# A four-layer kernel on one core: six blocks of attention's result are turned by VectorE and a scratch array in DRAM instead of TensorE, and the last seven-product group gets a third PSUM tile and a last product in column halves

## The chip, the cores and the metric

The kernel runs on one core of one Trainium2 chip. The metric is the device time of one execution in microseconds (us). The kernel before takes 1473.97 us, the median of three runs (1473.82 to 1475.48).

## What is computed

Activations of 8 batches of 128 tokens, width 512, all in f32, pass four layers. Each layer adds `ffn(cond(x))` to `x`:

```
x = x + L0_ffn(L0_cond(x))     # gated FFN with LoRA; expert LoRA with a router
x = x + L1_ffn(L1_cond(x))     # two low-rank layers
x = x + L2_ffn(L2_cond(x))     # attention over a paged cache; linear + routed low-rank
x = x + L3_ffn(L3_cond(x))     # two more routed low-rank layers
```

The change lies where the third layer's attention ends, and at the very end. Attention (32 query heads, 8 key heads, head width 128, up to 512 cached keys and 128 new ones) gives `y2`, 1024 tokens x 512. What follows needs `y2` turned, with features on the partitions:

```
H = y2 @ W.T + b;  z = y2 @ A
logits, weights = from every second token's H[:, 0:8] and z @ LiMEs.T   # softmax, top 2
y3 = H + ((z * (weights @ LiMEs)) @ Bmat) * scaling
```

The last layer ends with a product of 1024 tokens x 512 by a 512 x 512 matrix, added to `x` and written out.

## The kernel before, in words

**Layout.** `x` stays in SBUF, features on partitions, [128, 4, 1024]. `y2` is the other way round: [128 tokens, 8 batches, 512].

**Attention** (`run`, L1364 on) goes in 32 steps, `n`: 8 groups of heads (`qd`), and in each four pairs of batches (`p`). Step `n` weighs its pair (`weigh`: scores `st`, exponentials `pT` on ScalarE), projects the pair of step n+1 (`project`), and puts the result of step n-1 through the output weights (`leave`: products `wo`, added to `y2` by VectorE and GpSimd). Matrix products are done by the seven-product scheme (seven block products in place of eight, the sums of blocks by VectorE). The sums of a step's exponentials are inverted and spread over the partitions through DRAM (`inverted`: SyncE's two DMAs `sums` and `R`), and `divided` (`oT`) uses them a step later. Keys and queries are turned by VectorE's 32x32 transposes, a DMA to DRAM (`written`, L1167, four DMAs each) and a DMA back (`kT`, L1165; `qT` and `kTn`, L1202 and L1204).

**The ending.** In the last group of heads (steps 28 to 31) the blocks of `y2` that are complete are turned. At the end of steps 29, 30 and 31, L1462 calls `end.turn` for the two batches of the pair before. `turn` (L1843) makes four TensorE transposes (L1849) into one PSUM tile `y2T` and one copy to SBUF (L1850: ScalarE for an odd batch, VectorE for an even one). The last two batches are turned in `layer2`, at its start.

`Y2T` feeds four things. `product` (the tiles `h`: four quarters of the tokens, q = 0 to 3; one product is 32 matmul records), `anchors` (`hdT`, then `hd`, every second token of all quarters), `low` (`z`), and through `anchors` the `routing`: a row of small VectorE, ScalarE and GpSimd operations (L1874 to L1944) that ends in `p`, which TensorE transposes in `gains` (`pT`, L1952). `product(0)` is called in `run` before the last `leave`; `layer2` calls anchors, product(1), routing, product(2), gains, and so on in that order.

**What sets the order.** Inside attention most instructions are held in the order in which they are written (`kept`, `tc.keep_in_program_order`). `turn` and `layer2` are not: there a scheduler at build time moves instructions on each engine by its own costs, and the order so found is fixed in the program. Each engine, SyncE's DMA queue too, runs its instructions in that order. Loads of the last two layers' weights (`open3`: `Bm`, `W`, `Wq`, `keys`, `wB3T`, `wmr`, `BwT`) are queued on SyncE behind step 31's DMAs.

**The end of the program** (`layer3`, `last`, class `Seven`). Four groups of seven products, 256 columns each; a group has two PSUM tiles (banks), `even` and `odd`, with two results in each. `last` adds the four results to `x` on VectorE (L2223) and sends each out by a DMA of SyncE (L2224). Then every engine reads a flag (`redo_i`, L814), branches over a part that is not run here (L815), and waits for the outstanding DMAs.

Of the kernel before, what the change touches and what calls it, by code (L numbers as in the profile page):

```python
# [10 lines left out]
F32 = mybir.dt.float32  # L11
I32 = mybir.dt.int32
AF = mybir.ActivationFunctionType
ALU = mybir.AluOpType
# [3 lines left out]
P = 128  # L18
NB = 8
NT = NB * P  # L20
D = 512
DC = D // P
# [25 lines left out]
def forward(ctx: ExitStack, tc: tile.TileContext, a: dict, out: bass.AP):  # L48
    nc = tc.nc
    pe, act, dve, pool, sp = nc.tensor, nc.scalar, nc.vector, nc.gpsimd, nc.sync  # L50

    def mm(o, lhsT, rhs, start, stop):
# [14 lines left out]
    x = xpool.tile([P, DC, NT], F32, tag="x", name="x")  # L67

    w3T, wB3T, A2T = (
        nc.dram_tensor(n, shape, F32, kind="Internal").ap()  # L70
        for n, shape in (("w3_turned", (D, D)), ("wB3_turned", (D, P)), ("A2_turned", (32, D)))
    )
# [5 lines left out]
    late_weights.append((  # L78
        a["A2"].rearrange("(c p) r -> p c r", p=P), A2T.rearrange("i (c q j) -> q i c j", q=4, j=32)
    ))  # L80
    late_turned = w3T, wB3T, A2T

    c0 = ExitStack()
    w0 = c0.enter_context(tc.tile_pool(name="w0", bufs=1))
# [36 lines left out]
    for k in range(7):  # L121
        n = 1 << k
# [214 lines left out]
    with c0:  # L337
# [73 lines left out]
        h = w0.tile([P, NF, NT], F32, tag="h", name="h")  # L411
# [157 lines left out]
        kept = tc.keep_in_program_order  # L569
        with tc.issue_after(rows_known.ins):  # L570
            for g in range(TG):
                token_sums(g)
            A = weight_sums(1, second, dve)
# [4 lines left out]
        for f in range(1, NF):  # L578
            after = f + 1 < NF and weight_sums(f + 1, gate_weights(f + 1))
            gates_by_seven(f, A, itertools.islice(tabled, 15) if f < 3 else itertools.islice(angles, 3))  # L580
            A = after
# [134 lines left out]
    with psa:  # L716
# [49 lines left out]
        kept = nc.dram_tensor("kept_x", (P, DC, NT), F32, kind="Internal").ap()  # L766
# [18 lines left out]
        y2, end = att.run(late, end_of, bank, lambda: sp.dma_start(kept, x))  # L785
# [29 lines left out]
    with tc.If(redo > 0):  # L815
        sp.dma_start(x, kept)
        y2 = attention_any(tc, a, x, ident, lens, kvrow, part, ww, wop, ypool, eps, rows, chunks, mm)
# [24 lines left out]
def attention(tc, a, x, ident, lens, kvrow, part, ww, wop, ypool, sums, rot, eps, psa, c2, chunks, mm):  # L842
# [6 lines left out]
    nc = tc.nc  # L849
# [517 lines left out]
    def run(pool_, end_of, bank, keep):  # L1367
        late.append(pool_)
        y2 = Y[0]
        squares(1, "q", 0, range(REP))  # L1370
        keys_terms = rotate(1)
        squared(1)
        keys_terms()
        roots(1)
        gather(2, "k")
        rotated(1)
        normed(1)
        end, prepared = None, iter(())
        w_ops, wo_ops = iter(()), WO[0].factors()

        def some(ops, k=1):
            return lambda: [next(ops, None) for _ in range(k)]

        for n, (qd, p) in enumerate(steps):

            after = n + 1 if 0 < n < len(steps) - 1 else None
            weigh(n, 0)
            sums_of, outs = added(n, 0), iter(())
            if n == 1:
                some(wo_ops, 2)()  # L1390
            next(sums_of)
            (some(wo_ops) if n == 1 else some(w_ops))()
            every(sums_of)
            every(w_ops)
            if n:
                divided(n - 1)
                outs = outputs(n - 1)
                if not after:
                    every(outs)
            if after:  # L1400
                project(after, {
                    "u2": lambda: every(outs),
                    "c22": lambda: (turn_cached(2)() if n == 1 else None, some(wo_ops, 3)()),
                    "c11": lambda: (squares(after, "k", 0, (0,)), squares(after, "q", 0, (0, 1))),
                    "c12": lambda: squares(after, "q", 0, (2, 3)),
                })
                keys_terms = rotate(after)
                if n + 2 < len(steps):
                    if steps[n + 2][1] == 0:
                        weights(steps[n + 2][0])  # L1410
                    gather(n + 2, "k")
                leave(n - 1, {
                    "one": lambda: (
                        squares(after, "q", 1, range(REP)), squares(after, "k", 1, (0,)), roots(after),
                    ),
                    "c22": lambda: (every(wo_ops), keys_terms(), rotated(after), normed(after), turn(after)),
                })
                fetch(after)
                gather(after, "v")
            mixed = mix(n, 0)  # L1420
            left = (lambda: leave(n - 1),) if n and not after else ()
            weigh(n, 1, {2: (some(mixed), *left), 3: (some(mixed),), 4: (some(mixed, NC),)})
            sums_of = added(n, 1)
            next(sums_of)
            summed(n, 0)
            if n == 0:
                next(sums_of)
                gather(1, "v")
            every(sums_of)
            if n == 0:  # L1430
                turn_at_once(1)
            summed(n, 1)
            if 0 < n < len(steps) - 2 and steps[n + 2][1] == 0:
                w_ops = W[steps[n + 2][0]].factors()
            inverted(n, some(w_ops))
            if n + 2 == len(steps):
                end.load_w2()
                end.load_aw()
            if left:
                end.shifted()  # L1440
            if n == 0:
                every(tokens(2))
            if n == 5:
                prepared = end.prepare(bank, lambda shape, name: wk.tile(shape, F32, tag="xs", name=name, bufs=1))
            next(prepared, None)
            every(mix(n, 1))
            next(prepared, None)
            if n and p == 0:
                out_weights(qd)
                wo_ops = WO[qd].factors()  # L1450
            if 0 < n < len(steps) - 2:
                turn_cached(n + 2)()
                some(w_ops)()
                every(tokens(n + 2))
            if n == 3:
                kept(keep())
            if n == 4:
                end = end_of(kept)

            if qd == NQ - 1 and p:  # L1460
                for j in range(2):
                    end.turn(y2, 2 * (p - 1) + j, bank)  # L1462
        divided(n)
        every(outputs(n))
        end.product(0, ("st", "st"), bank)
        leave(n)
        return y2, end
# [311 lines left out]
def ending(  # L1779
# [15 lines left out]
    def slot(j):  # L1795
        return slice(j * 32, (j + 1) * 32)
# [47 lines left out]
    def turn(y2, b, bank):  # L1844
# [4 lines left out]
            pe.transpose(ps[:, c, :], y2[:, b, c * P : (c + 1) * P], ident)  # L1849
        (act.copy if b % 2 else dve.tensor_copy)(Y2T[0][:, :, b * P : (b + 1) * P], ps)  # L1850

    def quarter(q):
        return slice(q * NT // 4, (q + 1) * NT // 4)

# [205 lines left out]
    class Seven:  # L2060


        def __init__(self, name, bank, A, B):
            self.A, self.B = A, B
            self.even, self.odd = (bank("mm", [P, 2, 256], f"{name}_{i}") for i in range(2))
            self.p1, self.u = (
                L3.w3.tile([P, 256], F32, tag=f"seven_{n}", name=f"{n}_{name}", bufs=2) for n in ("p", "u")
            )
            self.c = {(0, 0): (self.even[:, 0], None), (0, 1): (self.odd[:, 1], self.u),
                      (1, 0): (self.even[:, 1], self.u), (1, 1): (self.odd[:, 0], self.p1)}  # L2070

        def into(self, o, l, r, start=False):
            for c in range(2):
                mmq(o, l[:, c, :], r[:, c, :], start and c == 0, False)

        def begin(self):
            self.into(self.even[:, 0], self.A[0], self.B[0], True)
            act.copy(self.p1, self.even[:, 0])

        def go_on(self):  # L2080
            a11, a12, a22, s1, s2, s3, s4 = self.A
            b11, b21, b22, t1, t2, t3, t4 = self.B
            u, p1, even, odd = self.u, self.p1, self.even, self.odd
            self.into(odd[:, 1], s1, t1, True)
            self.into(odd[:, 0], s2, t2)
            dve.tensor_tensor(u, odd[:, 0], p1, ALU.add)
            dve.tensor_tensor(p1, odd[:, 1], p1, ALU.add)
            self.into(even[:, 1], s3, t3)
            dve.tensor_tensor(p1, even[:, 1], p1, ALU.add)
            self.into(odd[:, 1], s4, b22)  # L2090
            self.into(even[:, 0], a12, b21)
            self.into(even[:, 1], a22, t4)

    S = {}

# [107 lines left out]

    def last_begun(g, k, bank):

        f = S["o", g, k] = Seven(f"o3_{g}_{k}", bank, S["b"][k], S["z", g])
        f.begin()

    def last(g, k):
        f = S["o", g, k]  # L2210
        f.go_on()
        for (i, j), (ps, more) in reversed(f.c.items()):
            o = 2 * k + i
            tok = slice(g * 512 + j * 256, g * 512 + (j + 1) * 256)
            t = x[:, o, tok]
            if more is not None:
                dve.tensor_tensor(t, t, more, ALU.add)
        for ij in ((1, 1), (0, 1), (0, 0), (1, 0)):
            ps = f.c[ij][0]
            o = 2 * k + ij[0]  # L2220
            tok = slice(g * 512 + ij[1] * 256, g * 512 + (ij[1] + 1) * 256)
            t = x[:, o, tok]
            dve.tensor_tensor(t, ps, t, ALU.add)  # L2223
            sp.dma_start(out[o * P : (o + 1) * P, tok], t)  # L2224

    def layer2(y2, bank, do=range(NB)):

# [24 lines left out]
    def layer3(bank, between=lambda behind: None):  # L2252
# [35 lines left out]

    return SimpleNamespace(
        prepare=prepare, load_w2=load_w2, load_aw=load_aw, turn=turn,  # L2290
        product=product, shifted=shifted, open3=open3, layer2=layer2, layer3=layer3,
    )


# [63 lines left out]
```

## Time and profile before

One execution was profiled. It took 1478.06 us, 4.09 us (0.28%) above the median of the runs; the span that its trace covers, from the first instruction to the last, is 1476.2 us.

| what | value |
|---|---|
| median of the runs / profiled execution / its span | 1473.97 / 1478.06 / 1476.2 us |
| granted TensorE clock, mean | 0.998 |
| busy: TensorE, VectorE, GpSimd, ScalarE | 99%, 72%, 58%, 38% |
| DMA, mean over the span | 119 GB/s |
| end of attention's step 31 and ending up to `pT` | 1324.86 to 1360.38 us |
| last matmul ends / last VectorE addition ends / last instruction ends | 1469.17 / 1469.96 / 1476.2 us |

In the lines of the trace, `PE` is TensorE (`PEld` its loading of weights), `DVE` VectorE, `ACT` ScalarE, `POOL` GpSimd, `SP` SyncE; a `q` behind the name means the engine's queue, where its DMA issues, waits and branches lie. `L1849` is a line of the kernel. `out<-in` names tiles, with numbers left out. A row of the timeline has a start, a duration, engine, line, operation, tiles, shape and count; square brackets hold the idle time ahead of it and who ended it. A row of a group has the count, then the shortest, median and longest duration in ns, then the first and last start. Matmuls overlap, so a row's duration may be longer than the distance to the next one. The product of two 128-row blocks with 256 columns stands as two records, a transpose as one.

### The profile page before, as it was taken

How to read it: one execution, taken by the hardware profiler on the slowest of the kernel's cores; microseconds unless marked ns; L12 is line 12 of the kernel's file. 1: busy time of each engine (PE TensorE's matmuls, PEld its weight loads, DVE VectorE, ACT ScalarE, POOL GpSimd, SP SyncE). 2: the span in 40 equal slices, each digit the busy share in tenths (PEclk: the TensorE clock that was granted, in tenths of full speed). 3: DMA queues.
4: the chain of work that ended last, by engine and by line, in shares of the span. 5: the costliest groups of instructions: out<-in, count | busy, mean ns of one | idle time of the engine just before them, and what ended most of it. 6: DMA issues, size and time to landing. Idle time of an engine off the chain costs nothing.

```text
span 1476.2 us, 17664 instructions
## 1 busy us (share of the span) xinstructions
PE 1462.2 (99%) x5348; PEld 922.4 (62%) x5348; DVE 1063.5 (72%) x2125; ACT 561.2 (38%) x1421; POOL 851.1 (58%) x877
## 2 busy tenths in 40 slices
PE   9999999999999999999999999999999999999998
PEld 7888787455555555555565555555555555657886
DVE  4565534488888887777778777777878888875575
ACT  1111201044545544454554445445544444532110
POOL 2232104477767777777677777767777776731310
PEclk9999999999999999999999999999999999999999
DMA  7411222214645544564454455444445544343001
GB/s 244 121 44 33 47 42 68 91 38 118 183 152 170 155 118 125 156 182 127 138 151 119 125 155 180 133 138 147 116 131 154 170 143 135 113 121 99 1 16 45
DMA packets 168808, 175.09 MB, mean 119 GB/s; under 512 B 64544, under 2 KB 138528, under 8 KB 168576
## 3 DMA queue, kind: packets, MB, share of 16 engines
q1 hardware_dynamic: 150528, 136.86, 32.0%
q0 software_dynamic: 17056, 36.49, 7.9%
q8 instruction: 45, 0.74, 0.2%
q10 hardware_dynamic: 1120, 0.52, 0.1%
q14 instruction: 59, 0.48, 0.1%
HBM read 131.40 MB, written 42.14 MB: 118 GB/s over the span
## 4 chain that ended last, share of the span: by engine, by line
PE 95%; DVE 2%; DMA 1%; issue 1%; ACT 0%; SPq 0%; POOL 0%; DVEq 0%
PE st L1214 18%; PE av L1266 18%; PE g L381 9%; PE q_six L1020 8%; PE q_one L1020 6%; PE q_five L1020 6%; PE wo_two L1020 6%; PE dn L381 5%; PE wo_one L1020 4%; PE wo_six L1020 4%; PE eo_l L53 3%; PE h L1799 2%; PE z L1799 2%; PE midp_l L53 1%; PE o L1799 1%
## 5 line engine op out<-in xcount | busy, mean ns | idle before, releaser
L963 POOL DMA_INDIRECT kn<-in_k_cache,kvrow_k x256 | 272.0, 1062 | 77.3 <-issue 70.5
L963 POOL DMA_INDIRECT vals<-in_v_cache,kvrow_v x256 | 267.9, 1046 | 73.6 <-issue 60.5
L1266 PE MATMUL av<-pT,vals 128*128 128x512 f32 x640 | 290.6, 592 | 0.2 <-DVE oT L1276 0.2
L1218 ACT ACTIVATE pT<-st,hide 128x512 f32<-128x512 f32 x256 | 176.0, 688 | 186.9 <-PE st L1214 160.1
L1214 PE MATMUL st<-qT,kT 128*128 128x512 f32 x512 | 236.1, 594 | 1.3 <-issue 0.9
L1266 PEld LDWEIGHTS av<-pT,vals 128*128 128x128 f32 x640 | 121.4, 190 | 153.1 <-issue 148.0
L1119 POOL TENSOR_TENSOR vq<-q,txq 128x256 f32<-128x256 f32 x128 | 121.2, 978 | 137.6 <-ACT sqq L1093 97.9
L1214 PEld LDWEIGHTS st<-qT,kT 128*128 128x128 f32 x512 | 96.3, 190 | 111.6 <-issue 103.3
L1234 DVE TENSOR_TENSOR part<-pT 128x512 f32<-128x512 f32 x128 | 88.3, 691 | 77.1 <-ACT pT L1218 64.9
L1020 PE MATMUL q_one<-q,x 128*128 128x384 f32 x256 | 93.0, 486 | 0.0
L1093 ACT ACTIVATE sqq<-q 128x128 f32<-128x128 f32 x252 | 78.2, 310 | 10.4 <-DVE q L1069 3.7
L1020 PEld LDWEIGHTS q_one<-q,x 128*128 128x128 f32 x256 | 48.5, 190 | 39.8 <-issue 14.3
L1020 PE MATMUL q_six<-q_s,xs_all 128*128 128x384 f32 x192 | 69.8, 486 | 0.0
L1074 ACT COPY q<-q_one 128x256 f32<-128x256 f32 x32 | 11.9, 372 | 151.7 <-PE q_one L1020 133.4
L1020 PE MATMUL wo_one<-o,oT 128*128 128x256 f32 x256 | 65.8, 379 | 1.0 <-ACT k L1074 1.0
L1214 PE MATMUL st<-qT,kTn 128*128 128x512 f32 x128 | 65.4, 592 | 0.0
L1020 PE MATMUL wo_two<-o_s,os 128*128 128x256 f32 x256 | 60.5, 379 | 0.0
L1218 ACT ACTIVATE pT<-st,rs 128x512 f32<-128x512 f32 x64 | 44.0, 687 | 38.5 <-PE av L1266 22.6
L1020 PEld LDWEIGHTS wo_one<-o,oT 128*128 128x128 f32 x256 | 48.6, 190 | 14.7 <-issue 2.0
L450 POOL TENSOR_TENSOR ws<-wu 128x256 f32<-128x256 f32 (+1 forms) x9 | 6.4, 714 | 87.8 <-DMA wu<-in_WuT 80.1
L1250 ACT COPY rows<-rows 32x32 f32<-32x32 f32 x96 | 20.7, 216 | 92.8 <-DVE rows L1245 79.1
L381 PE MATMUL g<-xs,ws 128*128 128x256 f32 (+1 forms) x240 | 55.1, 379 | 0.0
(462 smaller groups left out, 2804.9 us busy)
## 6 DMA issues: line engine op xcount, KB each, us to landing
turned_new<-qkt SPq DMA_DIRECT2D x120, 160.0 KB
turned_cached<-kt SPq DMA_DIRECT2D x128, 128.0 KB
kT<-turned_cached SPq DMA_DIRECT2D x32, 512.0 KB
R<-sums SPq DMA_DIRECT2D x32, 512.0 KB
qT<-turned_new SPq DMA_DIRECT2D x30, 512.0 KB
q<-in_WqT SPq DMA_DIRECT2D x8, 1024.0 KB
o<-in_WoT SPq DMA_DIRECT2D x8, 1024.0 KB
kn<-in_k_cache,kvrow_k POOLq DMA_INDIRECT x256
```

What stands on the lines that cost most here:

```text
L53: pe.matmul(o, lhsT, rhs, start=start, stop=stop)
L381: pe.matmul(o, lhsT, rhs, start=start, stop=stop, skip_group_check=True)
L963: kept(pool.indirect_dma_start(out=d[:, c, :], out_offset=None, in_=kc if what == "k" else vc, in_offset=bass.IndirectOffsetOnAxis(ap=kvro ...
L1020: kept(pe.matmul(o, l[:, c, :], r[:, c, :], start=start and c == 0, stop=c == 1, skip_group_check=True))
L1093: kept(act.activation(sq, S[n][m][:, j, i, :], AF.Square, accum_out=S[n]["ssq"][:, j, col : col + 1]))
L1119: kept(pool.tensor_tensor(to, t[:, b, :, hi : hi + 64], wx[:, b, lo : lo + 64].unsqueeze(2).to_broadcast(list(to.shape)), ALU.mult,))
L1214: kept(pe.matmul(ps, s["kT"][:, c, 4 * j : 4 * j + 4, :] if c < 4 else s["kn"][:, j], s["qT"][:, :, REP * j : REP * (j + 1), :].rearrange( ...
L1218: kept(act.activation(pT[:, c, :, :].rearrange("p i t -> p (i t)"), ps, AF.Exp, **(dict(bias=hide[:, b, c : c + 1]) if c < 4 else dict(bia ...
L1234: kept(dve.tensor_tensor(o, l, r, ALU.add))
L1250: kept(act.copy(rows[0:32, g, :], rows[32 * g : 32 * g + 32, 0, :]))
L1266: kept(pe.matmul(ps, v[:, c, :], pT[:, c, :, :].rearrange("p i t -> p (i t)"), start=c == 0, stop=c == NC - 1, skip_group_check=True,))
L1799: return pe.matmul(o, lhsT, rhs, start=start, stop=stop, skip_group_check=True)
```

## The change

First part, the turning. For the pairs of steps 29, 30 and 31 the change calls a new `turned_in` in place of `turn`. For each of the two batches VectorE transposes a [128, 512] block in 32x32 squares to a tile in the buffers of the cached keys (`kn`), and SyncE writes it with four DMAs to an internal DRAM array; then four DMAs for each batch read it back into `Y2T`. All of it is held in its written order. The last two batches are turned as before.

```diff
+        def y2_turned(p):
+            bs = (2 * p, 2 * p + 1)
+            end.turned_in(y2, bs, lambda name: kvp.tile([P, 4, DC, 32], F32, tag="kn", name=name))
...
             if qd == NQ - 1 and p:
-                for j in range(2):
-                    end.turn(y2, 2 * (p - 1) + j, bank)
+                y2_turned(p - 1)
...
+    def turned_in(y2, bs, tile_of_turned):
+        if not Y2T:
+            Y2T.append(early.tile([P, DC, NT], F32, tag="yT", name="y2T"))
+        for b in bs:
+            t = tile_of_turned(f"y2t_{b}")
+            kept(dve.transpose(t, y2[:, b, :].rearrange("p (c k i) -> p k c i", k=4, i=32)))
+            for q in range(4):
+                kept(sp.dma_start(
+                    late_turned[3][b, :, :, q], t[32 * q : 32 * q + 32].rearrange("i k c j -> i (k c) j")
+                ))
+        for b in bs:
+            for k in range(4):
+                kept(sp.dma_start(
+                    Y2T[0][slot(k), :, b * P : (b + 1) * P],
+                    late_turned[3][b, :, DC * k : DC * (k + 1)].rearrange("i c a j -> i c (a j)"),
+                ))
```

Second part, the end. The group with `g + k == 2`, the last one, is built `apart`: its sixth product has a PSUM tile of its own, its last product is made in two halves of 128 columns, and the result of that product is added and sent out in two halves, one by SyncE, one by ScalarE. In every group `odd` is now allotted ahead of `even`.

```diff
+            self.odd = bank("mm", [P, 2, 256], f"{name}_1")
+            self.even = bank("mm", [P, 2, 256], f"{name}_0")
+            self.one, self.six = self.even[:, 0], (
+                bank("mm", [P, 2, 256], f"{name}_2")[:, 0] if apart else self.even[:, 1]
+            )
...
-            self.into(even[:, 0], a12, b21)
-            self.into(even[:, 1], a22, t4)
+            self.into(one, a12, b21)
+            for h in (slice(0, P), slice(P, 2 * P)) if self.apart else (slice(0, 2 * P),):
+                self.into(six[:, h], a22, t4[:, :, h])
...
-            dve.tensor_tensor(t, ps, t, ALU.add)
-            sp.dma_start(out[o * P : (o + 1) * P, tok], t)
+            n = P if f.apart and ij == (1, 0) else 2 * P
+            for h, by in zip(range(0, 2 * P, n), (sp, act)):
+                ps = f.c[ij][0][:, h : h + n]
...
+                dve.tensor_tensor(t, ps, t, ALU.add)
+                by.dma_start(out[o * P : (o + 1) * P, tok], t)
```

## The prediction

> **What bounds the kernel now.** I read the page first, its shares and its chain. The first line here is the page's busy time by engine, the second the chain of work that ended last.
>
> ```profile
> PE 1462.2 (99%) x5348; PEld 922.4 (62%) x5348; DVE 1063.5 (72%) x2125; ACT 561.2 (38%) x1421; POOL 851.1 (58%) x877
> ...
> PE 95%; DVE 2%; DMA 1%; issue 1%; ACT 0%; SPq 0%; POOL 0%; DVEq 0%
> ```
>
> TensorE has no gaps to fill. Work taken from it shortens the kernel, as long as no wait opens behind it. So: what do the turned blocks cost TensorE? From the groups by tile, then from the chain in order of time:
>
> ```profile
> L1849 PE MATMUL y2T<-ident,y x32: 272/273/273, 1273.9 to 1347.5; 128*128 128x128 f32 x32
> ```
> ```profile
> 1274.07 0.87 PE y2T L1849 x8
> ...
> 1307.19 0.87 PE y2T L1849 x8
> ...
> 1331.73 0.87 PE y2T L1849 x8
> ```
>
> A transpose lasts 273 ns, but eight stand on the chain with 0.87 us, 109 ns each. Third, TensorE's timeline where the ending begins, and of the same stretch the VectorE rows at the two ends of the routing:
>
> ```profile
> 1351.41 0.33 PE L1873 MATMUL hd<-ident,hdTs 128*128 128x128 f32 x1
> 1351.58 8.80 PE L1799 MATMUL h<-y2T,WT 128*128 128x256 f32 x40
> 1360.21 0.60 PE L1952 MATMUL pT<-ident,p 128*8 128x128 f32 x4
> ```
> ```profile
> 1351.78 0.22 DVE L1874 TENSOR_TENSOR hd<-hd,b 128x64 f32<-128x64 f32 x1 [1.10 <-PE hd L1873]
> ...
> 1357.56 0.19 DVE L1944 TENSOR_TENSOR p<-p,s 128x32 f32<-128x32 f32 x1
> ```
>
> The routing runs from 1351.74 (hd's end) to 1357.75, 6.0 us of small operations, and TensorE does not notice: 40 records of `h` (8.64 us on the chain) lie between `hd` and `pT`. This cover is what the change touches. Fourth, SyncE's rows of a write and its read back in step 29, and the end:
>
> ```profile
> 1275.35 1.91 SPq L1169 DMA_DIRECT2D turned_cached<-kt  x4
> 1281.11 0.34 SPq L1165 DMA_DIRECT2D kT<-turned_cached  x1
> ```
> ```profile
> 1469.20 0.76 DVE L2223 TENSOR_TENSOR x<-o,x 128x256 f32<-128x256 f32 x2 [0.76 <-PE o L1799]
> ```
> ```profile
> L815 SPq EVENT_SEMAPHORE  x8: 17/17/17, 1472.7 to 1474.5; - x8
> ...
> L815 ACTq EVENT_SEMAPHORE  x1: 17/17/17, 1461.1 to 1461.1; - x1
> ...
> L815 DVEq EVENT_SEMAPHORE  x1: 21/21/21, 1473.0 to 1473.0; - x1
> ```
>
> After 1470 only output DMAs and the closing of the program remain; SyncE's last DMA wait ends at 1474.5, and 1.7 us later all is over.
>
> **Turning: what is removed.** 24 transposes, 3 x 0.87 = 2.61 us of TensorE, all on the chain; three copies of 0.69 us on VectorE and three of 0.59 us on ScalarE, beside it. A rule speaks here: the Trainium skill (TensorE: Matmul & The Clock Gate, Part 4: PE-mode transpose) gives some 275 ns to a transpose within a kernel. The trace's duration agrees, 273 ns, but its spacing is 109 ns: by the rule 24 would be worth 6.6 us, by the row 2.61. I take the row, since only the spacing is TensorE's time here.
>
> **What is added.** Six VectorE transposes of 128x512, priced by `kt<-kn` (same shape and strides) at 0.71 us, two a step. In step 29 they come behind the `xs` sums that end at 1277.0 and hold up step 30's first addition of `part`: it was at 1277.42, may now start at 1276.6 and will at about 1278.2. VectorE had 1.32 us idle at 1287.02 for a product of TensorE, so this is made up before anyone needs it: nothing. In step 30 they run at 1304.7 to 1306.1, where VectorE sat idle until 1307.66: nothing. In step 31 VectorE waits 3.00 us for `R` anyway: nothing. Without that slack each pair would cost 1.4 us.
>
> 48 DMAs on SyncE, 16 a step, 64 KB each. Row for the trip: `turned_cached`, first write issued 1275.35, last issued by 1277.26, landed by 1281.11, so 3.9 us from last issue to landing. I take 0.44 us per issue (median of L1169), as much for a read (0.34 to 0.63, rows `R` and `kTn`), and 4.0 us to land (`R` of step 31: issued 1331.89, used 1335.90). A trip then is 3.5 + 3.9 + 3.5 + 4.0 = 15 us. Who is queued behind it on SyncE? Step 29: begins 1281.5, last read issued by 1292.4; next is `turned_new` at 1296.1. Step 30: behind `WT` and `AwT` (2 MB), reads done by about 1325; next is `sums` at 1328.8. Step 31: behind `R`, begins 1330.5, lands at 1345.4 (1347 with 0.63 a read); behind it the last layers' weights move from 1332.3 to about 1341, some 9 us later, `W` landing near 1348 where `qwp` wants it at 1360, `Bm` wanted at 1366, `wmr` at 1376: nothing. GpSimd's queue is not passed.
>
> **What is moved.** The built program of the changed kernel has another order on TensorE: product(1), which stood half before and half after `hd`, now lies wholly before it (it fills where the scheduler expects the late block), and between `hd` and `pT` there is only
>
> ```
> h_0 (product 2, first half) x8     in place of     h_0 x4, h_1 x8, h_0 x8
> ```
>
> that is 16 records in place of 40: 16 x 0.216 = 3.46 us in place of 8.64. In time: product(0) starts at 1332.61 - 2.61 = 1330.0. To `hd` TensorE has all it had, plus 24 records of `h` (5.18 us), less the short waits for copies of `y2T` it had there (0.2): `hd` ends at 1351.74 - 2.61 + 5.18 - 0.2 = 1354.1. Routing takes 6.0 again, with 0.1 to wake TensorE: `pT` starts at 1360.2. In the kernel before it starts at 1360.38 on the chain. Of 2.8 us gained some 2.65 become a wait at `pT`; **the turning brings 0.2 us**. From there the order is as before. First matmul that needs step 31's block: `hdT` at about 1350.9, more than 3.9 us after the late landing. If the cover were there, the gain would be the whole 2.8.
>
> **The end.** TensorE waited 0.18 us for VectorE's `p_o` at 1466.30; a product moved ahead of it (it no longer shares a bank) fills this: -0.18. The halves cost TensorE nothing: 8 records at 109 ns (the transposes' spacing, same columns) for 4 at 216. In the built program both halves' additions wait for the last matmul of both, so they do not overlap with it; but the addition of (0,0), which waited with (1,0) before, is now done earlier. After the last matmul there remain two additions of 128x128 (row `vals`, 0.28 us, 0.2 to 0.34 apart), about 0.5 in place of 0.76: together VectorE ends 0.45 earlier, near 1469.5. SyncE's last four issues ran from 1468.14 to 1471.78, with one of 1.58 and one of 0.81 us; the last was ready at 1469.96 and issued from 1470.97. Now SyncE has the same four, the last ready sooner, and ScalarE, idle, issues the other half at once. The Trainium skill (DMA: Bandwidth & Descriptors, Issuing engines are not separate DMA queues) says a second issuer saves only issue time; that is all I count. If SyncE's slow issue stays, its last ends at about 1471.2 (gain 0.6), else at 1469.8 (gain 2.0). ScalarE becomes a new candidate: after its DMA it reads the flag (0.47) and branches; its branch took from 1458.6 to 1461.1, so it is through at 1473.0, not 1461.1, against SyncE's 1474.5 before: no more than 1.5 to gain. I take **1.1 us**, bounds 0 and 2.0; the ends differ by SyncE's slow issue, which no row explains.
>
> **The sum.** 0.2 + 1.1 = 1.3 us. Against the profiled execution: 1478.06 - 1.3 = 1476.8, span 1474.9. Its 4.1 us over the median are outside the sum; from the median, 1473.97 - 1.3 = 1472.7.
>
> **Rivals.** *The cover holds.* Routing ends earlier than I think, or TensorE finds the missing 2.6 us. For: VectorE and ScalarE are almost idle there. Against: the row of operations is serial, and the order is fixed. Then 2.8 + 1.1: 1470.1. *Slower: the turned block is late.* Step 31's trip lands late at `hdT`, and everything behind, routing and `pT` too, moves with it, us for us. For: the 512 KB `R`, 128-byte squares and 8 reads queue on one issuer behind a receipt. Against: 4 to 5 us of slack. It decides above 1352.2, where the 1.3 us are eaten; at 1355, 4.1 us after 1350.9, the time is 1476.8 to 1477.5. *The end gives nothing:* the slow issue falls on the last DMA, or ScalarE's branch comes last: 1473.8. *The change does not do what it says* is excluded for the transposes (gone from the built order), and holds for the halves' overlap, as said.
>
> **How the numbers follow.** Likeliest, 0.65: 1472.7. Cover holds 0.15, late block 0.10, dead end 0.10. Range 1470.2 to 1475.6: at its low end the cover with little of the end, at its high end a late block of 3 us. Faster or slower by over 0.2% (2.9 us, about what a measurement of this kernel can tell from no change): faster 0.15 (the cover), slower 0.10 (late block), within 0.75.
>
> **What would show it.** Profile after: no `y2T` on TensorE before 1340; product(0) at about 1330.0; `hd` near 1354; before `pT` an idle of 2.6 us put down to VectorE's `p`; `pT` near 1360. If idle lies before `hdT` and names a DMA, the late block is right; if `pT` starts near 1357.6, the cover held. SyncE: `turned_new` not later than before. End: ScalarE's row after the branch near 1473, last addition near 1469.3. I am wrong if a wait appears in steps 29 to 31, above all for `qT` or `R`, which I priced at nothing.

## The result and the profile after

The changed kernel takes 1477.24 us, the median of 22 runs (1472.62 to 1480.26), beside 1474.59 us for the kernel before on the same chip (22 runs). The ratio is 1.0015, with a 95% interval of 1.0009 to 1.0021: it is slower by about 2.2 us (the medians differ by 2.65), and the forecast was 1472.7 us. The profiled execution took 1479.46 us with a span of 1477.7 us.

The two executions drift against each other: ahead of anything that the change touches, the one after already runs 1.1 us earlier (the first scores with new keys of step 29, `st<-qT,kTn`, stand at 1266.18 before and at 1265.08 after). So I measure from that row, called K below, and not from the start of the span. `1360.19` after is K + 95.11; `1360.21` before is K + 94.03.

TensorE's work fell, as meant. The first fence is the page's busy time, the second the groups of tile `y2T`: eight transposes are left of 32, and 24 reads of the scratch array are new.

```profile
PE 1460.3 (99%) x5328; PEld 919.6 (62%) x5328; DVE 1066.9 (72%) x2129; ACT 559.5 (38%) x1418; POOL 853.3 (58%) x877
```
```profile
L1869 SPq DMA_DIRECT2D y2T<-y_turned x24: 309/432/501, 1286.1 to 1338.6; - x24
L1853 PE MATMUL y2T<-ident,y x8: 272/272/273, 1344.4 to 1346.4; 128*128 128x128 f32 x8
```

SyncE's rows of step 31 show the trip through DRAM: writes from 1329.51, reads until 1339.02, and the median read lands 2.1 us after its issue, so the block is there at about 1341.1, over 5 us ahead of `hdT` at 1346.62.

```profile
1329.08 0.34 SPq L1260 DMA_DIRECT2D R<-sums  x1
1329.51 5.35 SPq L1864 DMA_DIRECT2D y_turned<-y2t  x8
1335.37 3.65 SPq L1869 DMA_DIRECT2D y2T<-y_turned  x8
```

TensorE's timeline of the ending; below it, VectorE's first and last row of the routing.

```profile
1344.36 0.38 PE L1853 MATMUL y2T<-ident,y 128*128 128x128 f32 x2
...
1346.62 0.42 PE L1803 MATMUL hdT<-y2T,WH 128*32 128x128 f32 x4
1346.97 0.70 PE L1803 MATMUL h<-y2T,WT 128*128 128x256 f32 x2
1347.60 0.63 PE L1803 MATMUL z<-y2T,A 128*32 128x256 f32 x4
1348.16 2.86 PE L1803 MATMUL h<-y2T,WT 128*128 128x256 f32 x12
1350.94 0.99 PE L1803 MATMUL hdT<-y2T,WH 128*32 128x128 f32 x26
...
1353.71 0.33 PE L1895 MATMUL hd<-ident,hdTs 128*128 128x128 f32 x1
1353.88 3.62 PE L1803 MATMUL h<-y2T,WT 128*128 128x256 f32 x16
1360.19 1.01 PE L1974 MATMUL pT<-ident,p 128*8 128x128 f32 x4 [2.69 <-DVE p L1966]
1361.13 1.94 PE L1803 MATMUL qwp<-W,Wq 128*32 128x512 f32 x8
```
```profile
1354.08 0.23 DVE L1896 TENSOR_TENSOR hd<-hd,b 128x64 f32<-128x64 f32 x1 [1.68 <-PE hd L1895]
...
1359.85 0.19 DVE L1966 TENSOR_TENSOR p<-p,s 128x32 f32<-128x32 f32 x1
```

Three things are to be seen. Product(1) lies ahead of `hd`, mixed with `hdT` and `z`, and only 16 records lie behind it. TensorE then waits 2.69 us for VectorE's `p`. And after the wait the same instructions take nearly twice their time: `pT` 1.01 us in place of 0.60, `qwp` 1.94 (before: 1.07). The stretches of 1 us say why. Behind the length of a stretch stand the busy times of TensorE, its weight loads, VectorE, ScalarE and GpSimd; the third number from the right is the granted clock of TensorE.

```profile
1359.00:1360.00 1.00, 0.00 (x0) 0.00 (x0) 0.86 (x5) 0.00 (x0) 0.00 (x0) 1.00 0.00 0
1360.00:1361.00 1.00, 0.81 (x4) 0.37 (x4) 0.04 (x1) 0.00 (x0) 0.00 (x0) 0.57 0.00 0
1361.00:1362.00 1.00, 1.00 (x8) 0.22 (x11) 0.00 (x0) 0.57 (x1) 0.00 (x0) 0.50 0.00 0
1362.00:1363.00 1.00, 1.00 (x12) 0.34 (x8) 0.00 (x0) 0.00 (x0) 0.74 (x2) 0.50 0.06 16
1363.00:1364.00 1.00, 1.00 (x21) 0.41 (x14) 0.04 (x1) 0.75 (x2) 1.00 (x2) 0.72 0.00 0
```

A mean of 0.57 means half the clock for 0.86 us of the second row, and 0.72 for 0.56 us of the fifth: 0.86 + 1 + 1 + 0.56 = 3.42 us at half. In the kernel before it is 1.00 in all these stretches.

The end: VectorE's last additions, the issues of the output DMAs, and the closing rows.

```profile
1469.00 1.60 DVE L2252 TENSOR_TENSOR x<-o,x 128x256 f32<-128x256 f32 x5
```
```profile
L2253 SPq DMA_DIRECT2D out<-x x16: 332/382/1862, 1437.1 to 1472.5; - x16
...
L2253 ACTq DMA_DIRECT2D out<-x x1: 373/373/373, 1470.7 to 1470.7; - x1
```
```profile
L816 SPq EVENT_SEMAPHORE  x8: 17/17/17, 1473.5 to 1476.0; - x8
...
L816 ACTq EVENT_SEMAPHORE  x1: 17/17/17, 1474.3 to 1474.3; - x1
```

SyncE still has one slow issue, 1.86 us (1.58 before), and is again the last to be done, at 1476.0. The last matmul ends at 1470.07, and the span 7.63 us later; before these were 1469.16 and 7.04.

All kernels of this study by the same rows, in us, with their times. `y2T(6)` is TensorE's first transpose of the last two batches (1344.36 in the timeline above), `h<-zp` the first product behind `pT` that needs the routing's weights; columns give the time from the start of one row to the start of the next:

| kernel | `y2T(6)` to `hd` | `hd` to `pT` | `pT` to `h<-zp` | K to last matmul's end | after it | ratio to before (95%) |
|---|---|---|---|---|---|---|
| before | 6.02 | 8.80 | 5.96 | 202.98 | 7.04 | 1 |
| changed | 9.35 | 6.48 | 7.27 | 204.99 | 7.63 | 1.0015 (1.0009 to 1.0021) |
| changed, again | 9.36 | 6.48 | 8.96 | 206.66 | 5.75 | 1.0018 (1.0010 to 1.0025) |
| turning only | 9.36 | 6.48 | 8.96 | 207.33 | 7.12 | 1.0031 (1.0019 to 1.0043) |
| end only | 6.02 | 8.80 | 5.96 | 202.59 | 7.76 | 0.9995 (0.9987 to 1.0003) |
| order of the change only | 9.35 | 6.48 | 7.23 | 207.88 | 7.03 | 1.0030 (1.0017 to 1.0043) |
| changed, six products ahead of `pT` | 9.35 | 6.39 | 5.96 | 203.73 | 6.15 | 1.0016 (1.0009 to 1.0023) |
| turning only, six products | 9.38 | 6.39 | 5.95 | 204.14 | 5.42 | 1.0013 (1.0006 to 1.0021) |
| changed, three products | 9.35 | 6.40 | 5.93 | 203.63 | 7.36 | 1.0014 (1.0005 to 1.0022) |
| changed, not mixed | 8.07 | 6.49 | 5.94 | 202.41 | 6.05 | 1.0007 (0.9998 to 1.0017) |
| turning, order held | 6.02 | 8.80 | 5.96 | 200.45 | 5.53 | 0.9987 (0.9980 to 0.9995) |
| changed, order held | 6.02 | 8.80 | 5.95 | 199.96 | 7.02 | 0.9984 (0.9976 to 0.9992) |
| order held, ScalarE sends two | 6.02 | 8.80 | 5.95 | 200.02 | 6.72 | 0.9976 (0.9967 to 0.9986) |
| order held, not mixed | 5.91 | 8.37 | 5.95 | 199.49 | 7.06 | 0.9984 (0.9977 to 0.9990) |

### The profile page after: what moved, and what is told of

It is laid out like the page before. It is cut to its first block, busy times and chain, and to the rows that moved or that the text cites. A ratio compares the mean times of both kernels' runs of the same rounds, so it can differ in the third digit from the quotient of the medians.

```text
span 1477.7 us, 17710 instructions
## 1 busy us (share of the span) xinstructions
PE 1460.3 (99%) x5328; PEld 919.6 (62%) x5328; DVE 1066.9 (72%) x2129; ACT 559.5 (38%) x1418; POOL 853.3 (58%) x877
## 4 chain that ended last, share of the span: by engine, by line
## 5 line engine op out<-in xcount | busy, mean ns | idle before, releaser
L1094 ACT ACTIVATE sqq<-q 128x128 f32<-128x128 f32 x252 | 78.2, 310 | 11.6 <-DVE q L1070 4.9
```

What stands on the lines that cost most here:

```text
L1094: kept(act.activation(sq, S[n][m][:, j, i, :], AF.Square, accum_out=S[n]["ssq"][:, j, col : col + 1]))
```

## The experiments

**Theory T**: the turning saves its 2.6 us, and the order that the scheduler then finds loses more: the mixing, the wait at `pT`, and the half clock behind it. **Rival D**: the trip through DRAM loses, by its DMAs on SyncE. **Rival E**: the end loses.

**The turning alone**: the changed kernel with the end of the kernel before (class `Seven`, `last_begun` and `last` put back).

> The turning through DRAM alone, with the end of the kernel before. Theory T (the turning saves its 2.5 us on TensorE and loses more behind it: product(1) stands ahead of hd, so TensorE waits 2.7 us at pT, mixes 32- and 128-column products for some 0.9 us more, and runs at half clock after the wait for some 1.3 us): about 2 us slower than the kernel before, 1476.5, with the same idle of 2.7 us at pT and granted clock near 0.5 after it. Rival E (the end is what loses): about 2.3 us faster than before, near 1472. Rival D (SyncE's 48 more DMAs delay something): slower too, but with a wait that names a DMA in steps 29 to 31.

Measured 1481.28 us beside 1476.32, ratio 1.0031 (1.0019 to 1.0043): slower than expected, and by its ratio than the whole change, though the intervals meet. The idle at `pT` is there, 2.70 us, and from K on no wait of TensorE names a DMA, in this kernel or in any other of the study: D has nothing to stand on. What is larger in this trace is the stretch of half clock (columns as above):

```profile
1360.00:1361.00 1.00, 0.20 (x2) 0.20 (x3) 0.55 (x4) 0.00 (x0) 0.00 (x0) 1.00 0.00 0
1361.00:1362.00 1.00, 1.00 (x8) 0.29 (x9) 0.00 (x0) 0.50 (x1) 0.00 (x0) 0.63 0.00 0
1362.00:1363.00 1.00, 1.00 (x8) 0.20 (x4) 0.00 (x0) 0.07 (x1) 0.29 (x1) 0.50 0.06 16
...
1368.00:1369.00 1.00, 1.00 (x5) 0.89 (x5) 0.00 (x0) 0.00 (x0) 1.00 (x2) 0.95 0.00 0
```

It is 0.74 + 6 + 0.10 = 6.84 us long, twice 3.42. Here the Trainium skill (TensorE: Matmul & The Clock Gate, Part 1: The HAM clock gate) fits: it says that the clock follows TensorE's activity in a window of 3.4 us that runs freely, whatever the kernel does. The traces bear it out: in the changed kernel the half clock behind `pT` begins at 1360.15 and the one behind the last matmul at 1472.79, which is 33 times 3.413 us. In the window just ahead of the half clock TensorE was busy for 0.75 us of 3.41 in the changed kernel, for 0.71 us here (the length, TensorE's busy time, the clock):

```profile
1356.74:1360.15 3.41, 0.75 (x4) 1.00 0.00 0
```

One window at half clock cost 1.31 us from `pT` to `h<-zp` (7.27 - 5.96), two cost 3.00. Why it was one window there and two here, with TensorE busy again in both, is not shown. The page's advice is to avoid pauses over 3.4 us; here 2.69 us was enough, and the measurement decides. Over the runs the clock does not set the two kernels apart: its mean is 0.9978 in the six runs of this one and 0.9979 in the 22 of the changed kernel.

**The end alone**: the kernel before with the third PSUM tile and the halves (`Seven` and `last` are those of the change).

```diff
-        f = S["o", g, k] = Seven(f"o3_{g}_{k}", bank, S["b"][k], S["z", g])
+        f = S["o", g, k] = Seven(f"o3_{g}_{k}", bank, S["b"][k], S["z", g], g + k == 2)
...
```

> The third PSUM tile and the column halves alone, with TensorE's transposes. Theory T: within 0.6 us of the kernel before (0.4 us gained ahead of the last matmul, as much or a little more lost behind it). Rival E: about 2.5 us slower. The prediction on record: 1.1 us faster, near 1473.5.

Measured 0.9995 (0.9987 to 1.0003): as T said, no loss, and no more than 0.4 us of gain in the trace (202.59 for 202.98). Rival E is out.

**The order held**: the changed kernel in which TensorE's instructions around `hd` are pinned in the order of the kernel before. `held` is a function that makes `turn`, product(1), `hdT`, `z`, `hd` and product(2)'s first half one instruction at a time, by a list, each pinned behind the one before it. Three VectorE operations that test attention's sums (L799 to L801 in the kernel before) are held behind `zp`, where they stood there too.

```diff
-        end.layer2(y2, bank, do=range(NB - 2, NB))
+        behind_zp = end.layer2(y2, bank, do=range(NB - 2, NB), row=[('t6', 2), ('h10', 3), ('t6', 2), ('t7', 4),
+            ('hdT', 3), ('h10', 1), ('hdT', 13), ('z', 16), ('hd', 1), ('h10', 4), ('h11', 8), ('h20', 8)])
...
+        with tc.issue_after(behind_zp.ins):
```

> The changed kernel with TensorE's order around hd pinned to that of the kernel before: most of product(1) lies between hd and pT again. Nothing else is changed. Theory T: hd ends near 1349, pT starts near 1357.7 with no idle and the clock at 1.0, and the time falls by about 4.5 us against the changed kernel, to 2 us below the kernel before (about 1472.5). Rival D (the trip through DRAM is what loses): the wait moves to hdT and names a DMA, the time stays near 1477.

```profile
1344.83 0.33 PE L2298 MATMUL hd<-ident,hdTs 128*128 128x128 f32 x1
1344.99 8.80 PE L1804 MATMUL h<-y2T,WT 128*128 128x256 f32 x40
1353.63 0.60 PE L1975 MATMUL pT<-ident,p 128*8 128x128 f32 x4
1354.16 1.06 PE L1804 MATMUL qwp<-W,Wq 128*32 128x512 f32 x8
```

In TensorE's timeline the 40 records are back, no wait stands at `pT`, and `qwp` has its 1.06 us. From K to the last matmul it is 3.02 us shorter than before: 2.62 up to `y2T(6)`, by the transposes, and 0.39 by the end, so the trip through DRAM cost nothing in this stretch. The time is 1474.06 beside 1476.32, ratio 0.9984 (0.9976 to 0.9992). (The rows stand early in absolute time, since this execution's K is 4 us earlier, 1262.2.) Same DMAs, no loss: D is out as the cause.

**Useless work in the wait**: the changed kernel with six products that `pT` overwrites, so that TensorE is busy while VectorE makes `p`.

```diff
         pt = bank("mm", [P, NA, P], "pT2")
+        if fill:
+            for c in range(fill):
+                kept(mmq(pt[:, 0:2, :], W["2"][:, c % DC, 0:P], Y2T[0][:, c % DC, quarter(0)], True, True))
...
+        gaining = gains(bank, 6 if len(do) < NB else 0)
```

> The changed kernel with six extra products of 128x256 (W by y2T, 2.6 us, written to the PSUM tile of pT, where pT then overwrites them) between product(2)'s first half and pT: TensorE has work, useless work, while routing runs. Theory T: pT starts at the same time as in the changed kernel, the clock stays at 1.0 behind it, and the time is about 1.3 us less than the changed kernel's. If the slow stretch behind pT has another cause (data that come late): no change, or worse by what the products take.

In the trace it is as T said: `pT` comes no later (6.39 us after `hd`, 6.48 without), the clock stays at 1.00, and K to the last matmul is 1.26 us shorter. The mean clock over its 17 runs rose to 0.9986, but the time does not show it: 1.0016 beside 1.0015, and these were two chips. Since the window runs freely, one trace can be luck, so the same was done to the turning alone, where the clock had cost most.

> The turning alone (which was 4.6 us slower than before) with the six useless products between product(2) and pT. If the half clock behind the wait was what set it apart: the clock stays at 1.0, pT starts no later, and the time falls by 3.3 us against the turning alone, to about 1.2 us above the kernel before. If not the clock: as the turning alone, 4.6 us above.

TensorE's timeline of that kernel (the first row is the useless work):

```profile
1356.54 2.75 PE L1803 MATMUL pT<-y2T,WT 128*128 128x256 f32 x12
1359.31 0.60 PE L1977 MATMUL pT<-ident,p 128*8 128x128 f32 x4
1359.84 1.06 PE L1803 MATMUL qwp<-W,Wq 128*32 128x512 f32 x8
```

1.0013 in place of 1.0031, that is about 2.7 us less with 2.6 us of work more; 3.2 us in the trace (207.33 to 204.14). The intervals, up to 1.0021 and from 1.0019, touch only at their ends. The mean clock rose from 0.9978 to 0.9988 (16 runs), which is worth about 1.5 us of the 2.7. In the traces the loss behind `pT` was the clock, and not late data.

**The order of the change without the change**: the kernel before, with TensorE's transposes and the old end, and a list as above in the changed kernel's order, with the same three VectorE operations held.

```diff
+        row=[('h10', 6), ('t6', 2), ('h10', 2), ('h11', 1), ('t6', 2), ('t7', 4), ('hdT', 2), ('h11', 1),
+            ('z', 2), ('h11', 6), ('hdT', 14), ('z', 14), ('hd', 1), ('h20', 8)]
```

> The kernel before, with TensorE's transposes and the old end, and only TensorE's order around hd pinned to that of the changed kernel: product(1) wholly ahead of hd, with hdT and z mixed in. No trip through DRAM. Theory T (the order is what loses): the interval from y2T(6) to hd grows from 6.0 to about 9.3 us, pT waits about 2.7 us for VectorE's p, the granted clock falls to 0.5 behind it for one or two windows of 3.4 us as in the two kernels seen so far; 5 us slower than before with one window, 6.7 with two. Rival D (the DRAM trip or its DMAs lose): no slower than before, or by no more than the 0.9 of the mixing.

```profile
1357.04 0.33 PE L2269 MATMUL hd<-ident,hdTs 128*128 128x128 f32 x1
...
1363.52 1.01 PE L1953 MATMUL pT<-ident,p 128*8 128x128 f32 x4 [2.69 <-DVE p L1945]
1364.46 1.94 PE L1800 MATMUL qwp<-W,Wq 128*32 128x512 f32 x8
```

The same three marks in a kernel that makes no trip through DRAM: 9.35 us to `hd`, 2.69 us of wait, `qwp` at half clock. In the window ahead of the half clock TensorE was busy for 1.13 us. 4.90 us longer in the trace, as expected for one window; ratio 1.0030 (1.0017 to 1.0043). The order alone loses all that the change loses, and more than the transposes can pay.

**Not mixed**: the changed kernel with product(1) still ahead of `hd`, but `hdT` and `z` each in one piece. The middle of its list, beside that of the kernel just above:

```diff
-            ('hdT', 2), ('h11', 1), ('z', 2), ('h11', 6), ('hdT', 14), ('z', 14)
+            ('h11', 7), ('hdT', 16), ('z', 16)
```

> The changed kernel with product(1) still wholly ahead of hd, but hdT and z each in one piece instead of mixed with the 128-column products. Theory T: from y2T(6) to hd 8.6 us (6.0 and 12 more instructions of h at 0.216 us a record, 2.6) in place of 9.35, the wait at pT unchanged at 2.7, so 0.75 us sooner at pT. If it is not the mixing that cost 0.75: 9.3 us as in the changed kernel.

```profile
1349.83 1.12 PE L1804 MATMUL hdT<-y2T,WH 128*32 128x128 f32 x32
1350.77 1.91 PE L1804 MATMUL z<-y2T,A 128*32 128x256 f32 x32
1352.61 0.33 PE L2298 MATMUL hd<-ident,hdTs 128*128 128x128 f32 x1
...
1359.10 0.60 PE L1975 MATMUL pT<-ident,p 128*8 128x128 f32 x4 [2.70 <-DVE p L1967]
1359.62 1.06 PE L1804 MATMUL qwp<-W,Wq 128*32 128x512 f32 x8
```

8.07 us in place of 9.35: going to and fro between 32 and 128 columns costs 1.28 us in the changed kernel, more than the 0.75 expected, because the kernel before had 0.5 of it too (6.02 and 12 moved records of 0.216 would make 8.61). TensorE's weight loads in the changed kernel show where most of it lies. At each change between 32 and 128 columns the first load comes only after a pause and together with its matmul, while the loads within a group run ahead of theirs:

```profile
1346.62 0.14 PEld L1803 LDWEIGHTS hdT<-y2T,WH 128*32 128x32 f32 x4 [0.17 <-issue]
1346.97 0.30 PEld L1803 LDWEIGHTS h<-y2T,WT 128*128 128x128 f32 x2 [0.21 <-issue]
1347.60 0.14 PEld L1803 LDWEIGHTS z<-y2T,A 128*32 128x32 f32 x4 [0.33 <-DVE sums L2071]
1348.16 2.46 PEld L1803 LDWEIGHTS h<-y2T,WT 128*128 128x128 f32 x12 [0.41 <-issue]
1350.94 0.83 PEld L1803 LDWEIGHTS hdT<-y2T,WH 128*32 128x32 f32 x28 [0.33 <-issue]
```

These five make 1.45 us; in the kernel before there are three, of 0.70 us, and here one, of 0.33. (The gap that names VectorE's `sums` is the same 0.33 us, with no engine named, in the order of the change alone.)

And a surprise: after the same wait, 2.70 us, the clock stays up (`qwp` 1.06). In this trace the pause fell across the edge of two windows. Counted back from the half clock behind the last matmul (1470.64), the two windows are these, with TensorE busy for 1.81 and 2.19 us:

```profile
1354.59:1358.00 3.41, 1.81 (x9) 1.00 0.01 2
1358.00:1361.42 3.42, 2.19 (x29) 1.00 0.02 5
```

It doesn't always fall so: the mean granted clock over this kernel's 10 runs is 0.9981, beside 0.9989 in 33 runs of the kernel before.

**The changed kernel again**, on the chip of the next three.

> The changed kernel itself, so that the next three are compared with it on one chip. As on record: 0.15% (2.2 us) slower than before, with a wait of 2.7 us at pT. By the theory of the clock its runs differ among themselves by whole windows at half clock (1.7 us of loss each): some with none, some with one, some with two, so its mean granted clock over the runs is about 0.001 below that of the kernel before.

1479.24 us, 1.0018. Its profiled execution has two windows of half clock (8.96 us from `pT` to `h<-zp`) where the first had one; in the window ahead of them TensorE was busy for 0.72 us. The mean granted clock over its 21 runs is 0.9979, in the kernel before 0.9988 (64 runs). This mean also takes in the half clock behind the last matmul, when TensorE has nothing left to do: in the trace of the kernel before that is all of it, 4.8 us from 1471.39 on. So the clock of a single run says little, and in the kernel before, too, the runs at 0.998 take 0.9 us more than those at 0.999. If that last stretch is as long on average in both kernels, the difference, 0.0009 x 1479 = 1.3 us of TensorE's time, is an estimate of the mean price of the pause.

**Half the useless work.**

> The changed kernel with three useless products (1.3 us) ahead of pT in place of six: TensorE then waits 1.4 us. If a wait of 1.4 us is too short for the clock to fall: as with six products, the granted clock over the runs as in the kernel before (near 0.9988), the time about 1.3 us below the changed kernel's beside it. If any wait of more than a microsecond can bring the clock down: between the two.

Inconclusive on how short a pause is short enough. The scheduler moved two of the `qwp` products ahead of `pT`, so that the wait became 0.34 us:

```profile
1358.30 1.04 PE L1803 MATMUL qwp<-W,Wq 128*32 128x512 f32 x2
1359.69 0.60 PE L1977 MATMUL pT<-ident,p 128*8 128x128 f32 x4 [0.34 <-DVE p L1966]
```

It shows once more that the clock holds when the wait is gone (mean 0.9988 over 13 runs); its median lies 1.3 us below the changed kernel's beside it, 1477.90 and 1479.24, with intervals that overlap.

**The turning alone, with the order held.**

> The turning alone, with the end of the kernel before and with the order of the kernel before pinned. Theory T: the turning is worth its 24 transposes at 109 ns, and its DMAs and VectorE transposes cost nothing: from the scores of step 29 to the last matmul 2.6 us less than in the kernel before, and the time 2.6 us lower (0.9982).

2.53 us shorter from K to the last matmul, ratio 0.9987 (0.9980 to 0.9995). The same turning that lost 4.6 us in the scheduler's order gains about 2 in the old one.

**Two versions that go further.** In the first, the order is held and in the last group ScalarE sends the first two results and SyncE the last three; in the second, the order is held and `hdT` and `z` are in one piece.

```diff
-            for h, by in zip(range(0, 2 * P, n), (sp, act)):
+            for h, by in zip(range(0, 2 * P, n), ({(1, 1): (act,), (0, 1): (act,), (0, 0): (sp,), (1, 0): (sp, sp)})[ij] if f.apart else (sp,)):
```

> The changed kernel with the order pinned (as in order_held) and, in the last group, the first two results sent by ScalarE and the last three by SyncE. If the slow issue (1.6 to 1.9 us, on the second DMA of the last group in every kernel so far) belongs to SyncE's queue after a pause, it now falls on SyncE's second and the end is late by as much; if it belongs to the second transfer of the group, it falls on ScalarE and SyncE issues its three at once: the last DMA is issued some 0.8 us sooner after the last matmul than in the changed kernel, and the time is that of order_held less up to 0.8, about 3 us below the kernel before.

The groups of its output DMAs (count, then shortest, median and longest in ns):

```profile
L2254 SPq DMA_DIRECT2D out<-x x15: 332/382/1101, 1433.7 to 1468.3; - x15
...
L2254 ACTq DMA_DIRECT2D out<-x x2: 373/1010/1647, 1466.1 to 1466.6; - x2
```

Both queues now have a slow issue on their second DMA of the last group, ScalarE's of 1.65 us and SyncE's of 1.10, so neither of the two guesses was right. (Nor is it always the second: SyncE's second took 1.3 to 1.9 us in the other traces, not 1.6 to 1.9 as the expectation has it, and in the changed kernel's second trace the second took 0.38 us and the third 1.48.) The last issue ends 2.06 us after the last matmul (2.86 in the changed kernel), 0.8 sooner, yet what follows it varies by more than that from one execution to the next. Ratio 0.9976 (0.9967 to 0.9986), 3.5 us faster than the kernel before; it can't be told from the order held alone, whose interval overlaps.

> The changed kernel with the order pinned so that most of product(1) lies behind hd, as before, and hdT and z each in one piece (in the kernel before two records of h lay within hdT). In place of 6.0 us from y2T(6) to hd with four instructions of h there, 5.9 with five, since 0.5 us of going to and fro between 32 and 128 columns falls away; pT without a wait. 3.0 us from the order and the end, and 0.5: 3.5 us below the kernel before between the scores of step 29 and the last matmul.

The trace is as expected, 199.49, or 3.49 us less than before; the time is 0.9984 (0.9977 to 0.9990). Both versions are faster than the kernel before and than the changed one.

## Why the prediction was wrong

**Turning, removed: right.** 24 transposes at 109 ns were worth 2.6 us: in the four kernels with the order held, K to `y2T(6)` is 2.57 to 2.62 shorter than before.

**Turning, added: right in the sum, in parts by luck.** No wait for the block at `hdT`, `turned_new` issued at 1295.07 where I had 1296.1 (the 1.0 between them is the drift), no late block behind the trip. The trip of step 31 took about 11.6 us (1329.51 to 1341.1), not 15: eight writes 5.35 us where I took 3.5, but only 0.5 us from their end to the first read where I took 3.9, and 2.1 for a read to land where I took 4.0. The slack was smaller than I thought, too: the mixed `hdT` began at 1346.62, not at 1350.9, and with 15 us for the trip the block would have come 2 us ahead of it. No wait of TensorE for `qT` or `R`, which I feared, lies behind K in any of the traces.

**Turning, moved: the mechanism was right, one term wrong.** The order, the 16 records, the routing of 6.1 us and the idle of 2.6 us at `pT` (2.69) came as said. "Less the short waits for copies of `y2T` it had there (0.2)" is the term that failed: the mixing of 32- and 128-column products cost 0.74 us instead, 9.35 less 6.02 less 12 records of 0.216. So `pT` came not at the old time but 1.08 us after it (K + 95.11 for 94.03; that it stands near 1360 in both traces is the drift). The gain of 0.2 was a slip besides: I set a start of 1360.2 against 1360.38, where the chain lets `pT` begin, while the timeline's row has 1360.21, so like against like the gain was nothing. With the mixing priced at 0.74 in place of -0.2, the turning would have lost 0.9 us.

**"From there the order is as before": the step that failed, a term put at nothing.** The order was as before, the speed was not. I wrote that the 2.65 us "become a wait", and added 0.1 us to wake TensorE. The wait took the granted clock to half for one window or two: 1.31 us in the first execution, 3.00 in another, nothing in the one trace of a kernel with the same pause, and, by the estimate above, 1.3 us on average over the runs.

**The end: too high.** The product moved ahead brought its 0.18 us, and with the rest of the group 0.39 ahead of the last matmul's end, where I had summed 1.1 in all. Behind it VectorE did finish sooner, as forecast (0.53 us after the last matmul, 0.80 before), but SyncE's last issue did not (2.86 us after it, 2.62 before). SyncE's slow issue stayed, as my rival "the end gives nothing" had it, and in the five executions with the old end 5.4 to 7.1 us follow the last matmul, in the nine with the new form 5.8 to 7.8.

**The sum.** Predicted -0.2 and -1.1. Measured in the profiled execution: `pT` +1.08, clock +1.31, end -0.39, which is +2.00 (K to the last matmul's end: +2.01), and +0.59 behind it, +2.6; the medians differ by 2.65. So the start of `pT`, the clock and the end each missed by about 1.3 us; that the last of these, +0.59, is more than chance is not shown, for what follows the last matmul varies by over 2 us between traces. The rival "slower" named the right place, `pT`, for a wrong reason, a late block; its time, 1476.8 to 1477.5, was met by another mechanism. The rival "the cover holds" is what the kernel does once the order is held.

**What stays open.** Seven kernels with the trip kept their clock over their runs (the three with useless work, the four with the order held). In six of them the time lies 0.6 to 1.6 us above what K to the last matmul says (with six products: +0.75 us in the trace, ratio 1.0016), in one 0.6 below; in the two changed kernels without the trip (end only, order of the change only) it lies 0.3 to 0.5 below. So a cost of the trip of about 1 us outside that stretch isn't excluded. All of TensorE's waits for `qT` lie ahead of K, 0 to 2.2 us in these traces and 0.2 in that of before; such waits, or the scatter behind the last matmul, could make the difference, but no run shows it. How short a pause spares the clock, why the half clock lasts one window or two, and what makes an issue slow, isn't known either.

## What to carry to other kernels

When work is taken from the busiest engine, look first at what the scheduler does with the gap: pin the order of the kernel before and measure that too, for the turning alone gave 1.0031 in one order and 0.9987 in the other. A wait on TensorE is not paid by its length alone: a pause of 2.7 us can halve the clock for 3.4 or 6.8 us behind it, so leave independent products to cover a chain of small operations, even at the price of doing others later. And compare executions from a row that stands just ahead of the change: the two here had drifted by 1.1 us, nearly half of the effect.

## What the runs showed of the hardware

A pause of TensorE of 2.69 us was followed by a granted clock of 0.50 for 3.42 us, in other executions for 6.84 us or not at all; six products of useless work in the pause kept it at 1.00. On the grid of 3.41 us on which the clock changes, windows with 0.71 to 1.13 us of TensorE's work were followed by half clock, windows with 1.81 and 2.19 us were not. Going to and fro between products of 32 and 128 columns cost 1.28 us in one stretch of TensorE's program; at each change the first weight load stood idle for 0.17 to 0.41 us. In the last group one DMA of the issuing queue, in all traces but one its second, took 1.1 to 1.9 us to issue, on SyncE and on ScalarE alike, beside 0.33 to 0.37 for the first.
